# Conditional residual chain on one core: second gates and their difference in other slots, residual folded ahead of x's split, another order behind the last product

## The chip, the cores and the metric

The kernel runs on one core of one Trainium2 chip. The metric is the device time of one execution in microseconds (us); lower is better. Engines are named as in the profile: PE (TensorE) multiplies, DVE (VectorE) and ACT (ScalarE) work on tiles, POOL (GpSimd) folds residuals and issues accumulating DMAs, SP (SyncE) issues most other DMAs. A `q` behind a name means that engine's sequencer, which issues DMAs and waits.

## The reference

Four conditional layers, each added to its input, for eight sequences of 256 tokens and 1024 channels, all in float32:

```python
# L0: one weight W for all, plus a mixture of 8 rank-16 experts, top 2 by logits
logits = x @ Wr.T + 5 * one_hot(lang)         # per token
gates  = softmax over the two largest logits, 0 elsewhere
x = x + x @ W.T + 2 * sum_e gates[e] * (x @ A[e].T) @ B[e].T
# L1: a mask of signs per sequence
x = x + x @ W1.T + b1 + coeff[b] * (x @ (2 * mask[b] - 1))
# L2: one of 8 full weights per sequence
x = x + x @ W2[ids[b]].T
# L3: one of 8 rank-16 adapters per sequence
x = x + 16/16 * (x @ B3[ids[b]].T) @ A3[ids[b]].T
```

## The kernel before

**Split products.** Every float32 operand is split into a high part (`whi`, `ghi`, a cast to fp32r on ACT) and a low part (`wlo`, `glo`, the difference, on DVE). A product is hi·hi + hi·lo + lo·hi on PE. The residual "x +" is folded into the weights: `fold_block` adds the identity to a diagonal 128x128 block, so that x @ (W + I) comes out of PE.

**Order of the work.** The schedule is written by hand: each engine executes its instructions in the order in which the program emits them. The work is a list of slots. There are two passes, g=0 and g=1, each over two pairs of sequences, p0 and p1. A pass begins with the 16 slots of L0 (`l0_slot`), then come units of L1 and L2 (`unit_slot`), 64 in a pass. In L0 the 2x2 block product of both pairs is made with seven block products instead of eight (sums `S1` to `S4` of weight blocks, `T1` to `T4` of x blocks), two slots for each product. The parts C11, U1, V, W, C12, C22 and C21 leave PSUM in `l0_evacuate` (DVE row `c<-mm,c`, two tiles t=0, 1 of two column blocks each); slots 10 to 15 keep adding in the same PSUM banks after C12 has been read at the start of slot 12.

**What a slot emits.** In `l0_slot`, in this order: evacuations of earlier sums, the works listed for `-s`, the high parts of the items four ahead (`highs`, ACT), residual folds (`fold`, POOL), the low parts (`lows`, DVE), the works listed for `s`, merges of L1's weights (`merge_add`, POOL), PE's own products (`l0_main`), and last `merge_scale` (ACT, L257, which turns an int32 mask tile into scaled floats). Lists of works are built in `l0_works` with `at(slot, ...)`; a negative slot means ahead of that slot's high and low parts. High parts have five buffers and low parts four, so those of a slot can begin only when PE has finished the slot before.

**The gates.** `gates_by_rank(p)` brings the gates of a pair into the layout of ranks and tokens (tile `gt`). `gate(p)` multiplies them with the experts' hidden values from PSUM (DVE, `gt<-ph,gt`). `split_gates` makes `ghi` (ACT, L401) and `glo` (DVE). `gate_difference(g)` subtracts the second pair's from the first's (DVE, `gt<-gt,gt`) and splits the result. PE uses them as extra terms of products (`lora`): p1's in slots 9 and 13, the difference in slot 15.

**The head.** `head()` is slots 0 and 1 of the first pass, where everything waits for the first loads. It goes in four blocks (m = 2s + k): cast and split 512 columns of x, fold and cast and split 512 columns of `A11`, multiply, then experts on the same operand. SP's first issues (L1013 to L1020) bring x, `A11` and the experts' `la` in that order, before larger loads. Nine warm-up matmuls (L998) run meanwhile.

**The end.** After the last unit, L3 of the last sequence is left: `proj` (x times B3, PE), `sums` (row `pr`, which adds up four partial groups), `third` (its split `rt`, ACT and DVE), and the last product with A3, eight column blocks of 128 channels. `fill(2)` works off two pieces of the sequence before (`pf` on PE, an addition on DVE; the stores in `store()`). The residual of channels 4 to 7 is put into PSUM by PE with an identity matrix (L1050, L1055) and copied out by ACT (L1067); that of channels 0 to 3 is added by DVE (L1065). The stores are issued by SP, the last one of ACT's half by ACT (L1068 to L1070). `bank(n)` is one of four single PSUM banks, `ps.tile` a pair of banks.

Of the kernel before, what the change touches and what calls it, by code (L numbers as in the profile page):

```python
# [8 lines left out]
F32 = mybir.dt.float32  # L9
# [3 lines left out]
ALU = mybir.AluOpType  # L13
AX = mybir.AxisListType

P = 128
NB = 8
T = 256
N = 2 * T
# [15 lines left out]
def kernel(ctx: ExitStack, tc: tile.TileContext, x, lang, coeff, ids,  # L35
# [31 lines left out]
    def tt(o, a, b, op):  # L67
        nc.vector.tensor_tensor(o, a, b, op)  # L68
# [124 lines left out]
    def source(n):  # L193
        kind, q, m, j = items[n]
        if kind == "L0":
            return quad(q, m)[j]
        r = raws[n]
        return (f32(r) if kind == "L1" else r)
# [34 lines left out]
    def fold_block(t, eng=None):  # L233

        (eng or nc.gpsimd).tensor_tensor(t, t, ident, ALU.add)  # L235
# [37 lines left out]
    def prep_hi(n):  # L273
        if n not in his:
            his[n] = wp.tile([P, 1024], FR, tag="whi", name=f"whi{n}", bufs=HI_AHEAD + 1)
        return his[n]

    def prep_lo(n):
        if n not in los:
            los[n] = wp.tile([P, 1024], FR, tag="wlo", name=f"wlo{n}", bufs=LO_AHEAD + 1)  # L280
        return los[n]
# [116 lines left out]
    def split_gates(key, gt):  # L398
        hi = gp.tile([P, N], FR, tag="ghi", name="ghi", bufs=2)
        lo = gp.tile([P, N], FR, tag="glo", name="glo", bufs=2)  # L400
        copy(hi, gt)  # L401
        tt(lo, gt, f32(hi), ALU.subtract)
        gates[key] = hi, lo

    def gate(p):
        tt(gts[p], phs.pop(p), gts[p], ALU.mult)

    def gate_difference(g):

        a, b = (gts.pop(pair_of(g, j)) for j in range(2))  # L410
        tt(a, a, b, ALU.subtract)
        split_gates(("diff", g), a)
# [206 lines left out]
    def experts(g, p, n, k, kk):  # L619

        if k == 0:
            phs[p] = bank(3 - p % 2, f"ph{p}")
        v = [t.rearrange("p (k c) -> p k c", k=2) for t in (his[n], los[n])]
        hi, lo = (t[:, k % 4, :] for t in la_w[g, k // 4])
        mm(phs[p], hi, v[0][:, kk], start=(k == 0), stop=False)  # L625
        mm(phs[p], hi, v[1][:, kk], start=False, stop=False)  # L626
        mm(phs[p], lo, v[0][:, kk], start=False, stop=(k == K - 1))  # L627
# [14 lines left out]
    def la_parts(g, k0, k1):  # L642

        h = k0 // 4
        if (g, h) not in la_w:
            la_w[g, h] = [gp.tile([P, 4, P], FR, tag=tag, name=f"la{tag}", bufs=2)
                          for tag in ("ghi", "glo")]
        k = slice(k0 - 4 * h, k1 - 4 * h)
        raw = LA[g][:, k0:k1]
        hi, lo = la_w[g, h]  # L650
        copy(hi[:, k], raw)
        tt(lo[:, k], raw, f32(hi[:, k]), ALU.subtract)
# [16 lines left out]
    def l0_works(g):  # L669


        p0, p1 = pair_of(g, 0), pair_of(g, 1)
        w = {}

        def at(s, *fs):
            w.setdefault(s, []).extend(fs)

        def add(name, h, src):
            nc.gpsimd.dma_start(quad(g, name)[h], src, accum_op=ALU.add)

        def s1_add(h):
            fold_quad(quad(g, "S1")[h], h)
            add("S1", h, w0[1, 2 + h])

        def s3_add(h):
            t = quad(g, "S3")[h]
            copy(flat(t), flat(quad(g, "S2")[h]))
            fold_quad(t, h)
            add("S3", h, w0[1, 2 + h])

        def s4_add(h):
            copy(flat(quad(g, "S4")[h]), flat(quad(g, "S2")[h]))
            add("S4", h, w0[0, 2 + h])

        def less(h, name, j, i):

            t = flat(quad(g, name)[h])
            nc.scalar.mul(t, t, -1.0)
            add(name, h, x[pair_of(g, j)][:, 4 * i + 2 * h:4 * i + 2 * h + 2])

        def both(f, *args):
            return [lambda h=h: f(h, *args) for h in range(2)]

        def subs(o, a, b):
            return [lambda h=h: sub(g, o, a, b, h) for h in range(2)]

        def lb_parts():
            copy(lbs[0], lb_raw)
            tt(lbs[1], lb_raw, f32(lbs[0]), ALU.subtract)

        if g == 0:
            at(1, constants, *both(s1_add))
            at(2, *both(less, "T1", 1, 0), lambda: router([p0]))
            at(3, lambda: weigh([p0]), lambda: expand(p0), lb_parts, *subs("S2", "A11", "S1"))
            at(4, *both(s4_add), lambda: gate(p0))
            at(5, lambda: router([p1]))
            at(6, lambda: weigh([p1]), lambda: expand(p1))
        else:
            at(0, *both(s1_add), *both(less, "T1", 1, 0))
            at(2, lambda: expand(p0))  # L720
            at(3, *subs("S2", "A11", "S1"))
            at(4, *both(s4_add), lambda: gate(p0))
            at(5, lambda: expand(p1))
        at(-5, lambda: split_gates(p0, gts[p0]))
        at(4, *both(less, "T3", 1, 1))
        t2 = subs("T2", "T1", "B22")
        at(7, t2[0], *both(s3_add))
        at(8, t2[1], lambda: gate(p1), lambda: split_gates(p1, gts[p1]))
        at(11, lambda: gate_difference(g))
        for h in range(2):  # L730
            at(9 + h, lambda h=h: add("T4", h, x[p0][:, 4 + 2 * h:6 + 2 * h]))
        for i in range(4):
            at(12 + i, lambda i=i: split_c(p1, i))
        return w
# [90 lines left out]
    def head():  # L825

        chain(0, 0)
        for s in range(2):
            for k in range(2):
                parts = [(2 * s, 512 * k, 512 * k + 512), (2 * s + 1, 512 * k, 512 * k + 512)]  # L830
                if s + k == 0:
                    parts[1:] = [(1, 0, 256), (1, 256, 512)]
                for i, c0, c1 in parts:
                    m = 2 * s + k
                    if i % 2 and c0 <= 512 * k + m * P < c1:
                        fold_block(W0[0, "A11", s][:, k, m * P:(m + 1) * P], nc.vector)
                    c = slice(c0, c1)
                    copy(prep_hi(i)[:, c], flat(source(i))[:, c])  # L838
                    tt(prep_lo(i)[:, c], flat(source(i))[:, c], f32(his[i])[:, c],
                       ALU.subtract)  # L840
                la_parts(0, 2 * s + k, 2 * s + k + 1)
                if (s, k) == (1, 1):
                    leave = logits(1)
                    highs(4)
                    leave()
                product(s, 0, [k], start=(s == 0))
                experts(0, 1, 2 * s, 2 * s + k, k)
            folded.update((2 * s, 2 * s + 1))
        by_token(1)


# [160 lines left out]
    for h in range(2):  # L1012
        for k in range(2):  # L1013
            m = 2 * h + k
            load_x(0, 0, m, m + 1)
            for c in ((slice(0, 256), slice(256, 512)) if m == 0 else (slice(0, 512),)):
                nc.sync.dma_start(W0[0, "A11", h][:, k, c], w0[0, h][:, k, c])
            if m % 2 == 0:
                k0, k1 = m, m + 2
                nc.sync.dma_start(LA[0][:, k0:k1], la[:, k0:k1])  # L1020
# [20 lines left out]


    b = NB - 1
    proj(b, 1, 1)
    at = l3[b]
    xt = xts[b]
    half = K // 2
    tiles = [ps.tile([P, 2, N], F32, tag="mm", name=f"po{b}_{i}") for i in range(2)]
    ends = {half + m: tiles[m // 2][:, m % 2, :T] for m in range(half)}
    mm(ends[half], ident, xt[:, half, :], start=True, stop=False)  # L1050
    fill(2)
    store()
    sums.pop(b)()
    for m in range(half + 1, K):
        mm(ends[m], ident, xt[:, m, :], start=True, stop=False)  # L1055
    rt = third(b)
    firsts = bank(0, f"po{b}_0"), bank(2, f"po{b}_2")
    for m in range(half):
        for po, m2 in ((firsts[m // 2][:, m % 2 * T:m % 2 * T + T], m),
                       (ends[half + m], half + m)):  # L1060
            mm(po, at[:, m2 * P:(m2 + 1) * P], rt, start=(m2 < half), stop=True)

    for m0, m1 in ((0, 1), (1, 2), (2, 4)):
        xs = xt[:, m0:m1, :].rearrange("p m t -> p (m t)")
        tt(xs, firsts[m0 // 2][:, m0 % 2 * T:m0 % 2 * T + T * (m1 - m0)], xs, ALU.add)  # L1065
        for m in range(m0, m1):
            copy(xt[:, half + m, :], ends[half + m])  # L1067
        nc.sync.dma_start(out[b, :, m0:m1, :], xt[:, m0:m1, :])  # L1068
        queue = nc.scalar if m1 == half else nc.sync
        queue.dma_start(out[b, :, half + m0:half + m1, :], xt[:, half + m0:half + m1, :])  # L1070


# [55 lines left out]
```

## Time and profile before

| | us |
|---|---|
| median of three runs | 607.04 |
| lowest and highest run | 606.71, 608.16 |
| profiled execution, its own time | 608.14 |
| its span, first to last instruction | 605.9 |
| PE busy | 596.5 |
| DVE busy | 473.8 |
| ACT busy | 385.5 |
| POOL busy | 129.7 |
| mean granted PE clock | 0.999 |

A row of the timeline or of the chain of waits gives the start and the length in us, then engine, line, operation, tiles and shapes, and in brackets how long the engine was idle before it and what ended that. Matmul rows overlap, because PE works on several at once; the distance between their starts is their price: about 0.227 us for 128x512 in fp32r. Two-pass float32 matmuls show two rows each. L68 is the helper `tt`, which makes every DVE tensor-tensor operation, so these are told apart by their tiles. DMA rows on a queue are the time of issuing; the landing comes later.

### The profile page before, as it was taken

What the parts mean: (1) busy time and instruction counts of PE and PEld (TensorE: products, weight loads), DVE (VectorE), ACT (ScalarE), POOL (GpSimd) and SP (SyncE); (2) the same over time, 40 slices, a digit from 0 to 9 for tenths busy, and PEclk for the clock granted to TensorE, in tenths of its full rate; (3) what the DMA queues carried; (4) which work ended last, traced back from release to release, by engine and by line L of the source; (5) the groups of instructions that cost most, each with busy time, mean ns of one, the idle gap of its engine ahead of it and who ended that gap; (6) DMA issues with size and microseconds to landing.
All of it is one profiled execution on the core that took longest, in us unless ns stands there. A gap on an engine that the chain in (4) does not pass through costs nothing.

```text
span 605.9 us, 8943 instructions
## 1 busy us (share of the span) xinstructions
PE 596.5 (98%) x3244; PEld 499.7 (82%) x3244; DVE 473.8 (78%) x557; ACT 385.5 (64%) x456; POOL 129.7 (21%) x174
## 2 busy tenths in 40 slices
PE   8999999999999999999999999999999999999996
PEld 7777778888888888888778878788888888888885
DVE  5579688899699899586655785879968999977853
ACT  4667465687569797543553864658866788764431
POOL 0322250114121114122110224500422110421100
PEclk9999999999999999999999999999999999999999
DMA  8977794467684767599940799936757686747503
GB/s 282 341 192 167 167 241 149 176 229 269 203 301 179 269 249 277 209 350 321 269 70 20 164 248 209 266 104 209 278 196 256 209 285 236 290 161 235 184 1 138
DMA packets 39821, 130.22 MB, mean 215 GB/s; under 512 B 4834, under 2 KB 7010, under 8 KB 39010
## 3 DMA queue, kind: packets, MB, share of 16 engines
q1 hardware_dynamic: 35026, 112.62, 52.6%
q0 software_dynamic: 4608, 16.78, 15.3%
q8 instruction: 25, 0.41, 0.3%
q10 hardware_dynamic: 144, 0.26, 0.1%
q14 instruction: 18, 0.15, 0.1%
HBM read 121.25 MB, written 8.39 MB: 214 GB/s over the span
## 4 chain that ended last, share of the span: by engine, by line
PE 89%; DVE 4%; DMA 3%; issue 2%; ACT 2%; SPq 0%; DVEq 0%; ACTq 0%
PE po L531 38%; PE mm L599 23%; PE po L540 20%; DVE wlo L68 2%; DMA A<-in_w 2%; PE pf L470 1%; PE pb L442 1%; DMA x<-in_x 1%; PE pl L308 1%; PE ph L626 1%; PE ph L627 1%; PE ph L625 1%; DVE c L68 1%; DVE gt L68 1%; ACT ghi L401 0%
## 5 line engine op out<-in xcount | busy, mean ns | idle before, releaser
L531 PE MATMUL po<-hl,whi 128*128 128x512 f32 x1016 | 254.5, 392 | 0.0
L531 PEld LDWEIGHTS po<-hl,whi 128*128 128x128 f32 x1016 | 182.8, 189 | 32.7
L68 DVE TENSOR_TENSOR wlo<-raw,whi 128x1024 fp32r<-128x1024 f32 x128 | 160.6, 1265 | 1.1 <-issue 1.1
L540 PEld LDWEIGHTS po<-hl,wlo 128*128 128x128 f32 x1016 | 137.6, 190 | 11.3 <-issue 1.6
L288 ACT CAST whi<-raw 128x1024 fp32r<-128x1024 f32 x128 | 133.8, 1048 | 18.1 <-PE mm L599 8.4
L540 PE MATMUL po<-hl,wlo 128*128 128x256 f32 x1016 | 142.3, 283 | 0.0
L599 PE MATMUL mm<-whi,whi 128*128 128x512 f32 x224 | 88.9, 397 | 1.1 <-DVE c L68 0.9
L599 PE MATMUL mm<-wlo,whi 128*128 128x512 f32 x224 | 87.9, 392 | 0.0
L257 ACT ACTIVATE raw<-raw,negc,c 128x1024 f32<-128x1024 int32 x64 | 79.6, 1243 | 4.7 <-DMA raw<-in_mask 4.7
L235 POOL TENSOR_TENSOR raw<-raw,ident 128x128 f32<-128x128 f32 x72 | 54.0, 753 | 120.8 <-DMA raw<-in_w 96.8
L599 PE MATMUL mm<-whi,wlo 128*128 128x512 f32 x224 | 71.0, 392 | 0.0
L68 DVE TENSOR_TENSOR raw<-raw,w 128x1024 f32<-128x1024 f32 x56 | 69.0, 1231 | 1.9 <-issue 1.9
L235 POOL TENSOR_TENSOR w<-w,ident 128x128 f32<-128x128 f32 x28 | 31.1, 1109 | 168.4 <-DMA w<-in_w 118.3
L68 DVE TENSOR_TENSOR wlo<-x,whi 128x1024 fp32r<-128x1024 f32 (+1 forms) x38 | 45.6, 1210 | 16.2 <-issue 8.6
L599 PEld LDWEIGHTS mm<-whi,whi 128*128 128x128 f32 x224 | 42.3, 189 | 13.0 <-ACT raw L257 1.6
L599 PEld LDWEIGHTS mm<-whi,wlo 128*128 128x128 f32 x224 | 42.2, 188 | 9.5 <-DVE wlo L68 0.4
L288 ACT CAST whi<-A 128x1024 fp32r<-128x1024 f32 x26 | 27.3, 1051 | 35.3 <-PE mm L599 17.7
L599 PEld LDWEIGHTS mm<-wlo,whi 128*128 128x128 f32 x224 | 42.3, 189 | 8.6
L572 ACT COPY c<-po 128x512 f32<-128x512 f32 (+1 forms) x34 | 18.8, 552 | 45.9 <-PE po L540 45.9
L288 ACT CAST whi<-x 128x1024 fp32r<-128x1024 f32 x34 | 35.3, 1049 | 11.1 <-PE mm L599 8.8
L575 ACT ACTIVATE sum<-po,b_sb 128x512 f32<-128x512 f32 (+1 forms) x36 | 23.0, 640 | 28.7 <-PE po L540 28.7
L68 DVE TENSOR_TENSOR wlo<-A,whi 128x1024 fp32r<-128x1024 f32 (+2 forms) x31 | 35.6, 1151 | 4.3 <-ACT whi L838 2.5
(126 smaller groups left out, 516.2 us busy)
## 6 DMA issues: line engine op xcount, KB each, us to landing
raw<-in_mask SPq DMA_DIRECT2D x64, 512.0 KB, 5.4
raw<-in_w SPq DMA_DIRECT2D x64, 512.0 KB, 4.7
w<-in_w SPq DMA_DIRECT2D x28, 512.0 KB, 3.4
out<-c SPq DMA_DIRECT2D x29, 256.0 KB, 2.8
A<-in_w SPq DMA_DIRECT2D x14, 512.0 KB, 8.7
x<-in_x SPq DMA_DIRECT2D x6, 1024.0 KB, 8.0
A<-in_w POOLq DMA_DIRECT2D x12, 512.0 KB, 8.5
x<-in_x POOLq DMA_DIRECT2D x12, 512.0 KB, 8.3
```

What stands on the lines that cost most here:

```text
L68: nc.vector.tensor_tensor(o, a, b, op)
L235: (eng or nc.gpsimd).tensor_tensor(t, t, ident, ALU.add)
L257: nc.scalar.activation(f32(raws[n]), raws[n], AF.Identity, bias=negc[:, b:b + 1], scale=c2[:, b:b + 1])
L288: copy(prep_hi(i), flat(source(i)))
L308: mm(pl[c:c + 32, :], wrs[:, k, :], X[g][:, j, k, :], start=(k < 4), stop=(k >= 4))
L442: mm(pb[c:c + 32, j * T:(j + 1) * T], l3b[b][:, k, :], xts[b][:, k, :], start=(k < 4), stop=(k >= 4))
L470: mm(po[:, i * T:(i + 1) * T], at[:, (m + i) * P:(m + i + 1) * P], rt, start=True, stop=True)
L531: mm(po, hi[:, c], xhl[:, k, j].rearrange("p h t -> p (h t)"), start=(k == 0), stop=False)
L540: mm(po[:, :T], lo[:, c], xhl[:, k, j, 0, :], start=False, stop=(k == K - 1))
L572: copy(xs, po[:, :, T:])
L575: nc.scalar.activation(xs, po[:, :, T:], AF.Identity, bias=b1c)
L599: mm(*args, skip_group_check=True, **kw)
```

## The change

Three places. In `l0_works`, `gate(p1)` moves ahead of slot 8's high and low parts, the split of its result ahead of the second half of T2's difference, and the gate difference from slot 11 to slot 10. In `head`, the fold of the residual block is put ahead of x's low part in the first block, and A's columns are cast and split in halves of 256 in all four blocks (before: in the first only); the first block of `A11` is loaded in one transfer instead of two. At the end, the identity copies are made for channels 6 and 7 alone, after `fill`, `store` and `sums`; channels 0 to 5 are added by DVE from three single banks; the column blocks are multiplied in the order 0, 6, 7, 1, 2, 3, 4, 5; and ACT issues two stores of 256 KB, SP three.

```diff
@@ l0_works
-        at(8, t2[1], lambda: gate(p1), lambda: split_gates(p1, gts[p1]))
-        at(11, lambda: gate_difference(g))
+        at(-8, lambda: gate(p1))
+        at(8, lambda: split_gates(p1, gts[p1]), t2[1])
+        at(10, lambda: gate_difference(g))
@@ head
         for s in range(2):
+            v, w = 2 * s, 2 * s + 1
+
+            def high(i, k, c0=0, c1=512):
+                c = slice(512 * k + c0, 512 * k + c1)
+                copy(prep_hi(i)[:, c], flat(source(i))[:, c])
+
+            def low(i, k, c0=0, c1=512):
+                c = slice(512 * k + c0, 512 * k + c1)
+                tt(prep_lo(i)[:, c], flat(source(i))[:, c], f32(his[i])[:, c], ALU.subtract)
+
             for k in range(2):
-                parts = [(2 * s, 512 * k, 512 * k + 512), (2 * s + 1, 512 * k, 512 * k + 512)]
-                if s + k == 0:
-                    parts[1:] = [(1, 0, 256), (1, 256, 512)]
-                for i, c0, c1 in parts:
-                    m = 2 * s + k
-                    if i % 2 and c0 <= 512 * k + m * P < c1:
-                        fold_block(W0[0, "A11", s][:, k, m * P:(m + 1) * P], nc.vector)
-                    c = slice(c0, c1)
-                    copy(prep_hi(i)[:, c], flat(source(i))[:, c])
-                    tt(prep_lo(i)[:, c], flat(source(i))[:, c], f32(his[i])[:, c],
-                       ALU.subtract)
-                la_parts(0, 2 * s + k, 2 * s + k + 1)
-                if (s, k) == (1, 1):
+                m = 2 * s + k
+                block = W0[0, "A11", s][:, k, m * P:(m + 1) * P]
+                high(v, k)
+                if m:
+                    low(v, k)
+                fold_block(block, nc.vector)
+                high(w, k, 0, 256)
+                high(w, k, 256)
+                if not m:
+                    low(v, k)
+                low(w, k, 0, 256)
+                low(w, k, 256)
+                la_parts(0, m, m + 1)
+                if m == 3:
                     leave = logits(1)
                     highs(4)
                     leave()
...
@@ first loads
             load_x(0, 0, m, m + 1)
-            for c in ((slice(0, 256), slice(256, 512)) if m == 0 else (slice(0, 512),)):
-                nc.sync.dma_start(W0[0, "A11", h][:, k, c], w0[0, h][:, k, c])
+            nc.sync.dma_start(W0[0, "A11", h][:, k], w0[0, h][:, k])
@@ end
     b = NB - 1
+    at, xt = l3[b], xts[b]
     proj(b, 1, 1)
-    at = l3[b]
-    xt = xts[b]
-    half = K // 2
-    tiles = [ps.tile([P, 2, N], F32, tag="mm", name=f"po{b}_{i}") for i in range(2)]
-    ends = {half + m: tiles[m // 2][:, m % 2, :T] for m in range(half)}
-    mm(ends[half], ident, xt[:, half, :], start=True, stop=False)
     fill(2)
     store()
     sums.pop(b)()
-    for m in range(half + 1, K):
-        mm(ends[m], ident, xt[:, m, :], start=True, stop=False)
+    ends = ps.tile([P, 2, N], F32, tag="mm", name="ends")
+    by_act = (K - 2, K - 1)
+    for i, m in enumerate(by_act):
+        mm(ends[:, i, :T], ident, xt[:, m, :], start=True, stop=False)
     rt = third(b)
-    firsts = bank(0, f"po{b}_0"), bank(2, f"po{b}_2")
-    for m in range(half):
-        for po, m2 in ((firsts[m // 2][:, m % 2 * T:m % 2 * T + T], m),
-                       (ends[half + m], half + m)):
-            mm(po, at[:, m2 * P:(m2 + 1) * P], rt, start=(m2 < half), stop=True)
-
-    for m0, m1 in ((0, 1), (1, 2), (2, 4)):
+    leave = [bank(n, f"po{b}_{n}") for n in (0, 2, 1)]
+
+    def place(m):
+        return ends[:, m % 2, :T] if m in by_act else leave[m // 2][:, m % 2 * T:m % 2 * T + T]
+
+    for m in (0, *by_act, 1, 2, 3, 4, 5):
+        mm(place(m), at[:, m * P:(m + 1) * P], rt, start=(m not in by_act), stop=True)
+
+    for m0, m1, queue in ((0, 1, nc.sync), (1, 2, nc.sync), (2, 4, nc.sync), (4, 6, nc.scalar)):
+        if m0 == 4:
+            for i, m in enumerate(by_act):
+                copy(xt[:, m, :], ends[:, i, :T])
+            nc.scalar.dma_start(out[b, :, K - 2:K, :], xt[:, K - 2:K, :])
         xs = xt[:, m0:m1, :].rearrange("p m t -> p (m t)")
-        tt(xs, firsts[m0 // 2][:, m0 % 2 * T:m0 % 2 * T + T * (m1 - m0)], xs, ALU.add)
-        for m in range(m0, m1):
-            copy(xt[:, half + m, :], ends[half + m])
-        nc.sync.dma_start(out[b, :, m0:m1, :], xt[:, m0:m1, :])
-        queue = nc.scalar if m1 == half else nc.sync
-        queue.dma_start(out[b, :, half + m0:half + m1, :], xt[:, half + m0:half + m1, :])
+        tt(xs, leave[m0 // 2][:, m0 % 2 * T:m0 % 2 * T + T * (m1 - m0)], xs, ALU.add)
+        queue.dma_start(out[b, :, m0:m1, :], xt[:, m0:m1, :])
```

More of the change, by code (lines that the diff above doesn't have):

```diff
@@ L846, in head @@
                 product(s, 0, [k], start=(s == 0))
-                experts(0, 1, 2 * s, 2 * s + k, k)
-            folded.update((2 * s, 2 * s + 1))
+                experts(0, 1, v, m, k)
+            folded.update((v, w))
         by_token(1)
```

## Prediction, made before the change was run

> **What bounds the kernel now.** I read the page's busy shares and its chain first, to see whether anything but TensorE sets the time:
>
> ```profile
> PE 596.5 (98%) x3244; PEld 499.7 (82%) x3244; DVE 473.8 (78%) x557; ACT 385.5 (64%) x456; POOL 129.7 (21%) x174
> PE 89%; DVE 4%; DMA 3%; issue 2%; ACT 2%; SPq 0%; DVEq 0%; ACTq 0%
> ```
>
> TensorE is the bound nearly everywhere, and the change leaves its work alone apart from two small copies at the very end. So it can pay only where TensorE waits, or before its start and after its end. Second, the waits of TensorE's matmuls (total, times, longest) over the whole span:
>
> ```profile
> PE mm L599 <- ACT ghi L401: 0.9, 2, 0.5
> PE mm L599 <- DVE c L68: 0.9, 2, 0.4
> ```
>
> Two kinds of wait, each once per pass (g=0, g=1), and both belong to what is moved. Third, the chain of waits inside the first pass (start, length, what):
>
> ```profile
> 65.40 0.61 DVE gt L68
> 66.01 0.02 issue
> 66.03 0.63 ACT ghi L401
> 66.66 0.04 issue
> 66.70 11.29 PE mm L599 x47
> ...
> 84.93 0.69 DVE glo L68
> 85.62 1.14 DVE c L68
> 86.77 0.14 issue
> 86.90 5.25 PE mm L599 x22
> ```
>
> See who stands in front of TensorE: in slot 9 the gates' high part, made last in slot 8's works; at slot 12 the evacuation `c` of C12, held on VectorE's queue behind the gate difference. The time lost is read from the starts of the matmuls, not from the listed idle, since a late low part stretches the rows after it:
>
> ```profile
> 65.71 0.61 PE L599 MATMUL mm<-whi,wlo 128*128 128x512 f32 x2
> 66.70 0.73 PE L599 MATMUL mm<-ghi,lb 128*128 128x512 f32 x2 [0.38 <-ACT ghi L401]
> 67.43 0.50 PE L599 MATMUL mm<-glo,lb 128*128 128x512 f32 x1
> 67.77 0.40 PE L599 MATMUL mm<-whi,whi 128*128 128x512 f32 x1
> ```
>
> From 65.71 to 67.77 are five starts; the same five one column block later (68.72 to 69.87) take 1.15 us, here 2.06: 0.91 us lost. Last, the head (ScalarE's cast of the second block of A, then TensorE's first and third matmul on it), and the last store to be issued:
>
> ```profile
> 9.53 0.62 ACT L838 CAST whi<-A 128x512 fp32r<-128x512 f32 x1 [0.96 <-DVE A L235]
> ...
> 10.21 0.50 PE L599 MATMUL mm<-whi,whi 128*128 128x512 f32 x1
> ...
> 10.93 0.49 PE L599 MATMUL mm<-whi,wlo 128*128 128x512 f32 x1
> ```
>
> ```profile
> 601.85 0.46 SPq L1068 DMA_DIRECT2D out<-c  x1
> ```
>
> **Second pair's gates, slot 8.** VectorE's order was: two `c`, two low parts (1.14 us each), the T2 difference (1.14), gate (0.61), then ScalarE's `ghi` (0.63) and VectorE's `glo` (0.69). New: `c` ends at 61.91, gate to 62.5, low parts to 64.8, `glo` to 65.4, T2 to 66.55. ScalarE is free from 62.3, so `ghi` is there at 63.2. TensorE comes to slot 9 at 65.71 + 2x0.227 = 66.16 and asks for `glo` at 66.6. The wait goes, with 1.2 us to spare. What is pushed back: slot 9's low parts by 0.6 us (ready 64.8, wanted from 66.4), and T2, whose cast starts at 68.64 now and, with slot 9 earlier, at 67.2 (T2 ready 66.55). The int32 scaling (L257) queued behind `ghi` comes earlier. Saved: 0.91 us, and 1.01 in the second pass (359.91 to 362.07 is 2.16 for 1.15).
>
> **Gate difference, slot 11 to 10.** At slot 12 the starts 85.86 and 87.21 are three apart: 1.35 instead of 0.68, 0.67 lost; 0.66 in the second pass. VectorE has a hole from 79.12 to 80.67 in slot 10, where nothing can be split until TensorE frees a buffer. The difference goes there: 79.1 to 79.7 (0.69, or 1.01 as it was beside GpSimd's fold), `ghi` to 80.35, `glo` to 81.05. Slot 11's first low part slips from 80.67 to 81.05. Then C12's first evacuation waits only for TensorE's second column block (83.6 + 0.3): 83.9 to 85.1, against 86.31 where slot 12 wants the bank: 1.2 us to spare. The price is on ScalarE, in order: `ghi` now waits there until 79.7, so L257 slips from 77.13 to 80.35, and slot 11's cast of `A` from 80.66 to 81.5, its low part to 82.5-83.7; that lies in the spare time. GpSimd's fold of that raw tile slips from 80.78 to about 81.6, its accumulating DMA with it (10.0 us to landing); first casts of raw tiles come at 101.54, so 9 us cover it. T4's DMA in slot 10 waits for a low part that ends before the difference starts, so it stays; SP's queue is not passed. What is late next, if that cover were gone, is again `c` at slot 12, one for one.
>
> Gates together: 0.91+1.01+0.67+0.66 = 3.25; I take 3.1, since a switch of operands may keep a few hundredths each.
>
> **Head.** SP issues one transfer instead of two for the first block of A: everything behind it goes out 0.45 us earlier, until issues wait for older transfers to land (8.62 waits for a landing, for one). The two halves landed at 4.1 and 4.5; the whole lands at about 4.5. VectorE then folds at 4.5-4.8 instead of after x's low part (5.04-5.32). That would start TensorE at 5.3 instead of 5.81, but the warm-up matmuls hold it until 5.58: 0.2 us earlier. The rows there start 0.43 us apart until 7.25, and 0.227 after 7.6. The Trainium skill, "TensorE: Matmul & The Clock Gate", Part 1, says that the array runs at half rate until a free-running window of 3.4 us has been busy; by it an earlier start only puts more matmuls at half rate, and the switch moves by some 0.5 us from run to run whatever the change. By the start alone the sum would hold 0.2; by the rule, with the switch at a fixed time, 0.2 x 0.227/0.43 = 0.1. I take 0.1. At the second block the cast in halves counts: two halves take 0.71 us, so the first is out 0.36 us after 9.53, at 9.9 instead of 10.15, its low part (0.42) at 10.3 instead of 10.88. TensorE lost 0.08 before 10.21 and 0.38 until 11.27 (1.06 for three starts): 0.46, all gone. Sum 0.5; bounds 0.1 (landings decide) and 0.9 (landings 0.4 us earlier too). Later blocks are ready over 1 us before use, which covers the 0.09 us that halves cost on ScalarE. The shift survives: ScalarE's and VectorE's next jobs start on TensorE's releases, and the loads behind them have landed (A12 at 15.9, its cast at 19.95).
>
> **Tail.** TensorE's copies of four residual blocks (0.43 us each) become two, and the first no longer stands before `fill(2)`. Now: first copy 596.06, `pf` 596.41, VectorE's two `pf` additions 597.04-598.33, `rt` 598.36-598.78, last product 598.83. New: `pf` at 596.1, additions 596.7-598.0, `rt` to 598.45, product at 598.5: 0.33 us earlier. SP then had five issues of 0.48 us each, first 599.94, last 601.85. New: SP 599.6, 600.0, 600.5; ScalarE copies two blocks by 599.8, issues 599.9, and its second at 601.15 behind VectorE's fourth addition. By issues the end comes 0.7 us earlier. The trace says the engines were 0.85, 0.98 and 0.88 busy from 601 to 604 at 292 to 351 GB/s. The skill, "DMA: Bandwidth & Descriptors", Issuing engines are not separate DMA queues, speaks against the second queue: it saves only issue time, the same 16 engines carry the bytes. By bytes (1.05 MB at 340 GB/s, 3.1 us from 0.85 us after the first issue) the end moves with the first issue: 0.33. I take the middle, 0.5, because the engines were only 0.27 busy from 600 to 601, so earlier issues can fill some of that; bounds 0.2 and 0.8.
>
> **Sum.** 3.1 + 0.5 + 0.5 = 4.1 us. The profiled execution took 608.14 (span 605.9 and 2.2 around it) and lies at the top of 606.71 to 608.16; the median is 607.04. Its span should become 601.8; from the median, 602.9. No change can be told here within 0.3%, 1.8 us.
>
> **The rivals.** (A) One of the two gate waits is refilled by what is queued next: the `c` additions or low parts are slower beside GpSimd (1.22 becomes 1.49 at 81.82, 2.49 at 87.81). Against it, spare time is 1.2 us at both places. Kept: half of 3.1, so 604.5. (B) The head follows the landings and the tail the bytes: 0.1 + 0.3 + 3.1, so 603.6. For it: DMA is 0.95 to 1.07 busy from 7 to 12. (C) Both gate waits are refilled: only 1.0 is left, 606.0, no change. (D) Slower: ScalarE's queue. `ghi` in slot 10 blocks it until VectorE's difference is done, and L257, both casts of slot 11, their low parts and then C12's evacuation follow. It decides beyond 1.2 us of slip, one for one, twice; to eat the 4.1 and 1.8 more, `ghi` must be late by 1.2 + 5.9/2, over 4 us, in each pass: 609. VectorE would have to be stretched past double for that; its rows in 76 to 80 are 1.22. Nor can the change miss its aim: both waits name the moved instructions.
>
> **How the numbers follow.** All parts pay 0.65 (602.9); A 0.14; B 0.09; C 0.07; D 0.05. Faster 0.65+0.14+0.09 = 0.88, same 0.07, slower 0.05. The range takes main case, A and B with the bounds: low 3.25+0.9+0.8 and half a microsecond of run spread (1.45 between the runs shown), 601.5; high A with a small head and tail (0.1 and 0.2), 605.2.
>
> **What would show it.** Right: slot 9 with no idle before `mm<-ghi`; the difference's row in the hole of slot 10, `c` of slot 12 split into two rows with a wait on TensorE before the second; 0.227 us starts from the second block of the head; last issue near the old 601.85 less 4.3, on ScalarE's queue. Wrong: a new idle before L599 at slots 9 to 13, ScalarE's casts of slot 11 over 2 us late, or TensorE's start at 5.8 again.

## The result: 3.9 us faster, and the profile after

| | before | after |
|---|---|---|
| median of six runs, us | 607.35 | 603.41 |
| lowest and highest run | 606.71, 608.16 | 602.74, 605.13 |
| ratio (95% interval) | | 0.9937 [0.9921, 0.9952] |
| profiled execution, its own time | 608.14 | 603.36 |
| its span | 605.9 | 601.0 |

The gain is 3.9 us by the runs and 4.9 us by the pair of traces; where the difference between the two comes from is told further down. The page of after, busy shares and chain:

```profile
PE 593.1 (99%) x3240; PEld 499.1 (83%) x3240; DVE 474.2 (79%) x561; ACT 385.7 (64%) x457; POOL 135.2 (23%) x174
PE 97%; ACT 1%; DVE 1%; issue 0%; DVEq 0%; POOL 0%; POOLq 0%; ACTq 0%
```

No engine was given less to do, apart from four fewer rows on PE (two float32 identity copies, two rows each). DVE has four more rows. What went is time in which PE got no further. The page books 3.4 us of it as less busy time of PE and 1.5 us as less idle time, since rows that waited for a late operand were stretched and counted as busy, and the four rows at the end are gone. Of the waits of PE (total, times, longest), the two rows that carried the forecast are absent, and no other row of L599 waiting for ACT or DVE has come in their place. These are left:

```profile
PE warm L1010 <- POOL ident masks.py:199: 1.4, 1, 1.4
PE ph L626 <- DVE wlo L68: 0.3, 1, 0.3
PE po L1071 <- DVE rt L68: 0.3, 1, 0.3
```

Slot 9 in the timeline of PE (start, length; a row with x2 holds two starts):

```profile
64.97 0.62 PE L599 MATMUL mm<-whi,wlo 128*128 128x512 f32 x2
65.44 0.63 PE L599 MATMUL mm<-ghi,lb 128*128 128x512 f32 x2
65.91 0.39 PE L599 MATMUL mm<-glo,lb 128*128 128x512 f32 x1
66.14 0.40 PE L599 MATMUL mm<-whi,whi 128*128 128x512 f32 x1
```

The same five starts that took 2.06 us now take 66.14 - 64.97 = 1.17, with no bracket, so no wait. Slots 10 to 12 on DVE show why the second wait went too:

```profile
77.40 0.95 DVE L68 TENSOR_TENSOR gt<-gt,gt 128x512 f32<-128x512 f32 x1
79.04 0.69 DVE L68 TENSOR_TENSOR glo<-gt,ghi 128x512 fp32r<-128x512 f32 x1 [0.69 <-ACT ghi L401]
...
82.27 1.22 DVE L68 TENSOR_TENSOR c<-mm,c 128x1024 f32<-128x1024 f32 x1
84.87 1.23 DVE L68 TENSOR_TENSOR c<-mm,c 128x1024 f32<-128x1024 f32 x1 [1.38 <-PE mm L599]
```

The gate difference and its low part lie in the former hole of slot 10. C12's first evacuation now ends at 83.5, and the second one waits for PE (the bracket) instead of PE for it.

To find where the 4.9 us lie I took the start of the same matmul in both traces, step by step down the program. The lead of after grows at these places:

| stretch | lead at its end, us | gained in it |
|---|---|---|
| first product of the head (5.81 to 5.43) | 0.38 | 0.38 |
| rest of the head, to slot 7 of the first pass | 0.72 | 0.34 |
| slot 9, first pass | 1.65 | 0.93 |
| slot 12, first pass | 2.33 | 0.68 |
| second pass, before its slot 7 | 2.83 | 0.50 |
| slot 9, second pass | 3.84 | 1.01 |
| slot 12, second pass, until the last `proj` | 4.53 | 0.69 |
| the end | 4.87 | 0.34 |

Gates 3.31, head 0.72, end 0.34, and 0.50 at a place that the change does not touch.

### The profile page after: what moved, and what is told of

The parts are those of the page before. It is cut to its first block, busy times and chain, and to the rows that moved or that the text cites. A ratio compares the mean times of both kernels' runs of the same rounds, so it can differ in the third digit from the quotient of the medians.

```text
span 601.0 us, 8936 instructions
## 1 busy us (share of the span) xinstructions
PE 593.1 (99%) x3240; PEld 499.1 (83%) x3240; DVE 474.2 (79%) x561; ACT 385.7 (64%) x457; POOL 135.2 (23%) x174
## 4 chain that ended last, share of the span: by engine, by line
PE 97%; ACT 1%; DVE 1%; issue 0%; DVEq 0%; POOL 0%; POOLq 0%; ACTq 0%
PE po L531 39%; PE mm L599 30%; PE po L540 20%; PE pl L308 1%; PE pf L470 1%; PE pb L442 1%; PE ph L626 1%; PE ph L627 1%; PE ph L625 1%; PE warm L1010 1%; PE pb L489 0%; ACT x L698 0%; DVE c L68 0%; PE po L548 0%; PE pg L392 0%
## 5 line engine op out<-in xcount | busy, mean ns | idle before, releaser
L599 PE MATMUL mm<-whi,whi 128*128 128x512 f32 x224 | 88.6, 396 | 0.0
L599 PE MATMUL mm<-wlo,whi 128*128 128x512 f32 x224 | 87.9, 392 | 0.0
L235 POOL TENSOR_TENSOR raw<-raw,ident 128x128 f32<-128x128 f32 x72 | 60.5, 843 | 115.6 <-DMA raw<-in_w 100.8
L257 ACT ACTIVATE raw<-raw,negc,c 128x1024 f32<-128x1024 int32 x64 | 79.5, 1242 | 3.9 <-DMA raw<-in_mask 3.9
L599 PE MATMUL mm<-whi,wlo 128*128 128x512 f32 x224 | 70.8, 391 | 0.0
L599 PEld LDWEIGHTS mm<-whi,whi 128*128 128x128 f32 x224 | 42.2, 189 | 11.1 <-issue 1.1
L599 PEld LDWEIGHTS mm<-whi,wlo 128*128 128x128 f32 x224 | 42.2, 188 | 9.2 <-DVE wlo L68 0.2
L599 PEld LDWEIGHTS mm<-wlo,whi 128*128 128x128 f32 x224 | 42.2, 188 | 8.6
L68 DVE TENSOR_TENSOR c<-mm,c 128x1024 f32<-128x1024 f32 x20 | 24.4, 1221 | 21.8 <-PE mm L599 21.8
```

The costliest lines, as they stand in the source:

```text
L257: nc.scalar.activation(f32(raws[n]), raws[n], AF.Identity, bias=negc[:, b:b + 1], scale=c2[:, b:b + 1])
L599: mm(*args, skip_group_check=True, **kw)
```

## The experiments

**Each part alone.** The change has three parts in different places, so each was put on the kernel before by itself; a fourth run moves the gates of slot 8 and leaves the difference in slot 11.

```diff
 gates only (e1)
-        at(8, t2[1], lambda: gate(p1), lambda: split_gates(p1, gts[p1]))
-        at(11, lambda: gate_difference(g))
+        at(-8, lambda: gate(p1))
+        at(8, lambda: split_gates(p1, gts[p1]), t2[1])
+        at(10, lambda: gate_difference(g))
 head only (e2): the edits of head() and of the first loads, nothing else
 end only (e3): the edits behind the last product, nothing else
 slot 8 only (e4): as e1, but
+        at(11, lambda: gate_difference(g))
```

Gates only: 

> The kernel before with only the three lines of the gates changed (gate of p1 ahead of slot 8's parts, its split ahead of T2's second half, the difference in slot 10). Theory: the four waits of TensorE at slots 9 and 12 are independent of head and tail, so the trace loses 0.9 + 0.7 in the first pass and 1.0 + 0.7 in the second: span 605.9 - 3.3 = 602.6, time 607.3 - 3.3 = 604.0. Rival 1 (a wait is refilled where the head is late): half of it, 605.7. Rival 2 (the 0.5 us that the changed kernel's trace gains between 296 and 312, on the load of la for the second pass, belongs to the moved gates): 603.5. If instead that load only jitters, the gain there comes or goes at random between these runs.

Head only: 

> The kernel before with only the head changed (one load of the first block of A, fold ahead of x's low part in the first block, casts and splits in halves in all four). Theory: TensorE reaches slot 2's products 0.7 us earlier and keeps it: span 605.2, time 606.6, and the starts come down to 0.23 us apart by about 6.8 us, not 7.3. Rival (the head's lead is used up by a later wait, on a load or on the gates of p0 at slot 5): below 0.2 us at the end, 607.2.

End only: 

> The kernel before with only the end changed (two identity copies instead of four, product order 0 6 7 1 2 3 4 5, stores by two queues). By bytes: the end follows the first store's issue, 0.4 us, span 605.5, time 606.95. By issues: it follows the last store's issue, 0.7 us, span 605.2, time 606.65. A rival that the tail gives nothing (the last store's landing is the same): 607.3.

Slot 8 only: 

> The kernel before with the second pair's gate and split moved in slot 8, the difference left in slot 11. Theory: the waits at slot 9 go (0.9 and 1.0), the waits at slot 12 stay at 0.7 each: span 604.0, time 605.4. Rival (TensorE's earlier start of slot 9 makes the wait at slot 12 longer, since VectorE's list of slot 11 then ends later against it): the wait at slot 12 grows to over 1.0 and the gain is below 1.3, time 606.0.

| run | median, us | ratio to before (95%) | span | slot 7 to slot 13, first pass | same, second pass |
|---|---|---|---|---|---|
| before | 608.09 | 1 | 605.9 | 35.06 | 41.02 |
| gates only | 604.38 | 0.9938 [0.9919, 0.9957] | 601.0 | 33.32 | 39.28 |
| slot 8 only | 605.61 | 0.9960 [0.9942, 0.9977] | 603.6 | 34.01 | 39.99 |
| head only | 607.55 | 0.9995 [0.9983, 1.0007] | 605.0 | 35.05 | 41.05 |
| end only | 607.30 | 0.9991 [0.9979, 1.0004] | 604.3 | 35.05 | 41.05 |
| whole change | 603.41 | 0.9937 [0.9921, 0.9952] | 601.0 | 33.45 | 39.32 |

The median of before in this table was taken beside the four runs; its span and stretches are of the trace shown at the start, and the ratio of the whole change is to its own before, 607.35. The last two columns run from the same matmul of `pg` in slot 7 to the first `ghi` product of slot 13. They hold only the gates' two places, and head and end leave them alone to 0.03 us. Slot 8 alone takes 1.05 and 1.03 off them, gates only 1.74 in each pass, the whole change 1.61 and 1.70 (why 0.13 less in the first pass is open). So both moves pay, each at its own place. In the waits of PE of slot 8 only, the row of `ghi` is gone and this one has stayed:

```profile
PE mm L599 <- DVE c L68: 0.9, 2, 0.4
```

In head only both rows have stayed:

```profile
PE mm L599 <- ACT ghi L401: 0.9, 2, 0.5
PE mm L599 <- DVE c L68: 0.9, 2, 0.4
```

Head and end alone are too small to be told from no change by their runs: the intervals of both contain 1, head only came to 607.55 where 606.6 was expected, and gates only gains nearly as much by its runs (3.7 us) as the whole change (3.9). Their size has to come from the traces.

**What in the head pays.** Two runs take one thing out of the changed head: the halves of A's columns behind the first block (e5), and the fold ahead of x's low part (e6). e7 puts all stores of the end on SP; in the head it is the same as after.

```diff
 whole columns again behind the first block (e5)
-                high(w, k, 0, 256)
-                high(w, k, 256)
+                cuts = ((0, 512),) if m else ((0, 256), (256, 512))
+                for cut in cuts:
+                    high(w, k, *cut)
 (the same for low)
 fold behind x's low part again (e6)
                 high(v, k)
-                if m:
-                    low(v, k)
+                low(v, k)
                 fold_block(block, nc.vector)
...
-                if not m:
-                    low(v, k)
```

> The changed kernel with A cast and split in one piece in blocks two to four of the head (halves kept in the first). Theory (the halves take TensorE's stall at the second block away): the second block's first three matmuls come 0.33 and 0.39 us apart again, as in the three traces of whole casts that are not held by TensorE itself, 0.25 to 0.4 us lost there; everything else as in the changed kernel. Rival (the block is reached late anyway because the half-rate matmuls of the first block last longer): starts 0.23 us apart, nothing lost.

> The changed kernel with the first block's fold behind x's low part again (one load and halves kept). Theory: the fold then starts at about 4.9 instead of 4.64 and TensorE's first product at 5.6 to 5.7 instead of 5.4; of these 0.2 to 0.3 us nothing or 0.1 is left at the second block, which waits for its own loads. Rival (the earlier fold is what shortens the head): the second block's first product moves by the same 0.2 to 0.3.

One execution each: 604.62 (whole columns) and 603.11 (fold behind), spans 602.1 and 600.8. The head is read from five times in each trace: the first product, the first start that the next one follows 0.23 us later (full rate), the start of x's low part in the second block (it follows the landing of that block of x by about 0.7 us), and the first `pl`, with which the head ends; the last column is the distance between these two.

| run | A's columns, blocks 2 to 4 | first product | full rate from | second block of x | `pl` | last two |
|---|---|---|---|---|---|---|
| before | whole | 5.81 | 7.62 | 8.61 | 17.48 | 8.87 |
| end only (e3) | whole | 5.77 | 6.11 | 7.81 | 16.71 | 8.90 |
| slot 8 only (e4) | whole | 5.71 | 6.05 | 8.27 | 17.18 | 8.91 |
| e5 | whole | 5.66 | 7.48 | 8.43 | 17.34 | 8.91 |
| after | halves | 5.43 | 6.75 | 8.20 | 16.63 | 8.43 |
| e6 | halves | 5.99 | 6.44 | 8.15 | 16.59 | 8.44 |
| e7 | halves | 5.42 | 6.41 | 8.07 | 16.50 | 8.43 |
| gates only (e1) | whole | 5.63 | 6.98 | 7.53 | 16.61 | 9.08 |
| head only (e2) | halves | 5.41 | 7.60 | 7.55 | 16.80 | 9.25 |

In the seven upper rows PE waits for the data of the second block, and the last column has two values only: about 8.90 with whole columns, 8.43 with halves. Three more traces with halves, of runs that come further down, give 8.42 (e9), 8.44 (e10) and 8.42 (e11). So the halves are worth 0.46 us where PE waits for the second block. The fold's place is worth nothing here: with it put back, the first product is later by 0.56 us (5.99 against 5.43) and `pl` is not (16.59 against 16.63). In the two lower rows the second block had landed early, and in e2 the full rate came late as well: PE itself was late then, and halves could not help. The second block of the head, in after and then in e5:

```profile
9.12 0.71 ACT L834 CAST whi<-A 128x256 fp32r<-128x256 f32 x2 [0.96 <-DVE A L235]
9.58 0.50 PE L599 MATMUL mm<-whi,whi 128*128 128x512 f32 x1
...
10.15 0.39 PE L599 MATMUL mm<-whi,wlo 128*128 128x512 f32 x1
```

```profile
9.36 0.62 ACT L834 CAST whi<-A 128x512 fp32r<-128x512 f32 x1 [0.96 <-DVE A L235]
...
10.03 0.50 PE L599 MATMUL mm<-whi,whi 128*128 128x512 f32 x1
...
10.76 0.50 PE L599 MATMUL mm<-whi,wlo 128*128 128x512 f32 x1
```

In after the cast is in two halves. The first `mm` starts 0.46 us after the cast begins (0.67 in e5, 0.68 in before), and the third one 0.57 us after the first (0.73 and 0.72). No landing is earlier for the one transfer in place of two: the low part of x's second block starts at 8.06 on average in four traces with the old loads and at 8.06 in eight with the new, between 7.53 and 8.61.

**The stores of the end (e7).** Both queues against one:

```diff
-    for m0, m1, queue in ((0, 1, nc.sync), (1, 2, nc.sync), (2, 4, nc.sync), (4, 6, nc.scalar)):
+    for m0, m1, queue in ((0, 1, nc.sync), (1, 2, nc.sync), (2, 4, nc.sync), (4, 6, nc.sync)):
...
-            nc.scalar.dma_start(out[b, :, K - 2:K, :], xt[:, K - 2:K, :])
+            nc.sync.dma_start(out[b, :, K - 2:K, :], xt[:, K - 2:K, :])
```

> The changed kernel with all five last stores issued by SP. From the last projection's last matmul to the end of the span the kernel before takes 10.9 us, the changed one 10.5. By issues: the last store is issued 0.5 us later than now, so 10.9 to 11.0. By bytes: first store at the same time, end 10.5 to 10.7.

603.29 in one execution, span 601.1. From the first matmul of the last `proj` (`pb` in the timeline) to the end of the span it is 10.91 to 10.99 in the four traces with the old end, 10.53 to 10.61 in seven with the new one (10.58 in after), and 10.89 here: of the 0.36 us that the new end gains on average, nearly all is lost again. The issues of the end in after, and then in e7:

```profile
595.09 1.41 SPq L1080 DMA_DIRECT2D out<-c  x3
595.20 0.37 ACTq L1077 DMA_DIRECT2D out<-c  x1
596.62 0.34 ACTq L1080 DMA_DIRECT2D out<-c  x1
```

```profile
594.85 1.30 SPq L1080 DMA_DIRECT2D out<-c  x3
596.24 0.41 SPq L1077 DMA_DIRECT2D out<-c  x1
596.74 0.41 SPq L1080 DMA_DIRECT2D out<-c  x1
```

After issues ACT's first store 0.11 us behind SP's first; in e7 it comes 1.39 us behind it. Counted from `pb`, the first store goes out at the same time in both (4.64), the last one 0.36 later in e7. So it is the second queue that pays, some 0.3 us, and not the new order of the products by itself.

**How much spare time C12's evacuation has (e9).** Rival D and rival A rest on the 1.2 us of slot 12. This run puts work in front of it: slot 11's low part of `A` is made three times instead of once, so two further subtractions of 128x1024 stand ahead of `c` on DVE. They write the same values again.

```diff
         at(10, lambda: gate_difference(g))
+
+        def again():
+            i = first[slot_of[g, 11]] + LO_AHEAD
+            tt(prep_lo(i), flat(source(i)), f32(his[i]), ALU.subtract)
+
+        at(11, *[again] * 2)
```

> The changed kernel with two more VectorE operations in slot 11 (the low part of slot 12's A made again, twice, 1.14 us each), in the place that the gate difference had. Theory: 1.2 us is spare ahead of slot 12, so C12's first evacuation ends about 1.1 us late and TensorE waits 1.0 to 1.2 us at slot 12 in each pass: span 2.2 us longer than without them. Rival (TensorE's wait there was set by ScalarE's split and not by VectorE's queue): no wait at slot 12, same span.

609.07 in one execution, span 606.7: 5.7 us more than after, where I had expected about 2.2. DVE, then PE, in slots 11 and 12 of the first pass:

```profile
80.91 4.74 DVE L68 TENSOR_TENSOR wlo<-A,whi 128x1024 fp32r<-128x1024 f32 x3 [0.26 <-ACT whi L288]
85.58 2.34 DVE L68 TENSOR_TENSOR c<-mm,c 128x1024 f32<-128x1024 f32 x2
```

```profile
84.00 0.61 PE L599 MATMUL mm<-whi,wlo 128*128 128x512 f32 x2
86.94 0.77 PE L599 MATMUL mm<-whi,whi 128*128 128x512 f32 x1 [2.32 <-DVE c L68]
87.50 0.63 PE L599 MATMUL mm<-wlo,whi 128*128 128x512 f32 x1
87.93 0.63 PE L599 MATMUL mm<-whi,whi 128*128 128x512 f32 x1
```

Two things were larger than I had counted. The three subtractions take 4.74 us, some 1.56 each from start to start instead of 1.14, and the slow ones have GpSimd's folds beside them (POOL is busy the whole of 82 to 84 in the windows below). The second of the three by itself:

```profile
82.17 2.08 DVE L68 TENSOR_TENSOR wlo<-A,whi 128x1024 fp32r<-128x1024 f32 x1
```

That GpSimd is the cause rests on more than this place: in before, after and e9 every low part of this size that took over 1.3 us had POOL busy beside it (33, 29 and 32 rows), and every one without POOL took 1.21 to 1.23. More than half of those beside POOL are not slow, though; what tells them apart is open. So `c` is 3.5 us later than in after, and PE stands still: the start that was due at 84.46 comes at 86.94, 2.48 us late. Then the starts are 0.43 apart instead of 0.227. The windows (length, then busy time of PE, PEld, DVE, ACT and POOL, then the granted clock, the share of DMA and GB/s) show why:

```profile
82.00:84.00 2.00, 2.00 (x10) 1.66 (x9) 1.97 (x2) 0.97 (x1) 2.00 (x4) 1.00 0.98 262
84.00:86.00 2.00, 0.62 (x3) 0.19 (x1) 1.97 (x3) 1.67 (x2) 1.59 (x3) 1.00 1.05 209
86.00:88.00 2.00, 1.06 (x3) 0.90 (x4) 2.00 (x3) 1.50 (x3) 1.17 (x3) 0.65 1.09 215
88.00:90.00 2.00, 2.00 (x6) 1.59 (x5) 2.00 (x2) 1.02 (x1) 0.00 (x0) 0.50 1.04 246
90.00:92.00 2.00, 2.00 (x10) 1.62 (x9) 1.33 (x2) 0.00 (x0) 0.00 (x0) 1.00 1.05 274
```

The granted clock (last column but two) falls to 0.50 at 86.6, while PE still stands, and is back at 90.0. The whole loss of the first pass, by the starts of the same matmul here and in after, is 4.02 us: the gap and some 1.5 us of half rate. In the second pass the same edit makes `c` 2.82 late and PE waits only 1.61:

```profile
382.36 0.47 PE L599 MATMUL mm<-whi,whi 128*128 128x512 f32 x1 [1.61 <-DVE c L68]
```

There the clock stays, and 1.88 is lost. What was taken up without loss is 3.5 - 2.48 = 1.0 in the first pass and 2.82 - 1.88 = 0.94 in the second: this is the spare time of slot 12.

**A further step (e10), with after run again beside it (e11).** In after, PE still waits 0.3 us for a low part in slot 2 of the first pass (`ph`, in its waits above), and in slot 5 two starts of `ghi` and `glo` stand too far apart. e10 makes the low parts of the items four ahead right behind their high parts at the end of the head, and puts the difference T3 one slot later in the first pass. e11 is after, unchanged.

```diff
 e10
                     highs(4)
+                    lows(4)
                     leave()
...
-        at(4, *both(less, "T3", 1, 1))
+        at(5 - g, *both(less, "T3", 1, 1))
```

> The changed kernel once more, as the reference for the next one on the same chip and for another trace of the same head. Theory: ratio 0.993 to 0.995; the head's length differs by up to 0.8 us from the first trace of it, since the clock's step to full rate and the landing of the second block of x fall at other times; the gates' waits stay away.

> The changed kernel with two more moves in the first pass: the low part of slot 2's x made in the head (VectorE is idle there) instead of behind the experts' low parts, and the negation of x for T3 (two ScalarE operations, 1.9 us, with their accumulating DMAs) in slot 5 instead of slot 4, behind the split of p0's gates. Theory: TensorE's waits at slot 2 (0.3 to 0.7 us) and at slot 5 (0.5 us) go, 0.8 to 1.2 us in all, and nothing else waits: ratio to the kernel before 0.992. Rival (T3's sums land late, or ScalarE's list of slot 5 is then too long for slot 6): a new wait of TensorE in slots 6 to 12, no gain over the changed kernel.

| run | median, us | lowest and highest | ratio to before (607.6 on this chip) | span |
|---|---|---|---|---|
| after again (e11) | 603.90 | 603.41, 605.54 | 0.9940 [0.9925, 0.9954] | 601.9 |
| e10 | 603.12 | 602.12, 603.55 | 0.9924 [0.9910, 0.9937] | 599.8 |

The two intervals overlap, so that e10 beats after is likely and not shown. Its wait in slot 2 is gone, and slot 5 runs evenly, but behind slot 5 a new wait stands, for ACT's copy of C11. The row is of PE's weight loads, and the two starts after it are 0.46 us apart instead of 0.23:

```profile
PEld mm L599 <- ACT c L744: 0.5, 1, 0.5
```

```profile
46.75 0.39 PE L599 MATMUL mm<-glo,lb 128*128 128x512 f32 x1
47.21 0.49 PE L599 MATMUL mm<-whi,whi 128*128 128x512 f32 x1
```

In the stretch with slots 5 and 6 the net gain is 0.2 us, where a stall of 0.6 had been removed. Here a wait did take the place of the removed one.

## Why the prediction was right, step by step

**Gates: 3.1 forecast, 3.31 measured.** The terms were 0.91, 1.01, 0.67 and 0.66; the stretches show 0.93, 1.01, 0.68 and 0.69. The four terms sum to 3.25, and the forecast put 3.1 without saying why; the 0.15 taken off was not needed. The orders worked out also hold: with the lead of 0.72 at slot 7 and 1.65 behind slot 9 taken into account, `gate`, `glo`, the difference, L257 and the cast of `A` lie within about 0.3 us of where they were put. The slip on ScalarE that was the price of the move was really paid, and hidden: its L257 of slot 10 starts only behind `ghi`, on time for slot 11:

```profile
78.39 0.62 ACT L401 CAST ghi<-gt 128x512 fp32r<-128x512 f32 x1 [2.80 <-DVE gt L68]
78.91 1.24 ACT L257 ACTIVATE raw<-raw,negc,c 128x1024 f32<-128x1024 int32 x1
80.06 1.04 ACT L288 CAST whi<-A 128x1024 fp32r<-128x1024 f32 x1
```

**The spare time: 1.2 forecast at slot 12, 1.0 and 0.94 measured (e9).** The forecast counted up to PE's start; in after `c` ends at 83.49 and PE starts at 84.67, 1.18 later, but in e9 some 0.2 us lie between the end of `c` and the start that waited for it. The error is too small to have decided anything, and rival A did not come. But the price of rival D beyond that point, "one for one", was too low: in the first pass the gap of 2.48 us brought some 1.5 us of half rate on top. So it was not D's mechanism but its price that was mis-sized. That ScalarE's `ghi` itself were late was not tried; e9 delays the same evacuation from VectorE's side.

**Head: 0.5 forecast, made of 0.46 for the halves and 0.1 for the earlier start.** The 0.46 is what the traces above give (8.90 against 8.43). For the earlier start nothing is to be seen: TensorE starts at 5.41 to 5.43 in after, e2 and e7 instead of 5.63 to 5.81, yet e6 starts at 5.99 and loses nothing. With the same first block as after, e5 starts at 5.66, so the start varies by itself as much as the change was to move it. The upper bound, landings 0.4 us earlier, is not borne out by the mean of 8.06 in both groups: in this part issues that went out earlier did not land earlier, as rival B had it. What the forecast had not in its sum is the spread of the head itself. In ten of the twelve traces `pl` follows x's second block by one of the two distances above, so the spread is that of the landing. The clock's step moves far more than the 0.5 us that the forecast named (see the last section), but it had a part in the length of the head only where the block came early (e2). The mean of `pl` is 17.00 in the four traces with the old head and 16.62 in five with the whole new one (after, e2, e7, e9, e11), 0.38 apart, inside a spread of 0.9 in the old ones. Before's own trace had the longest head of all: of the 0.85 us between its `pl` and that of after, 0.41 is the later second block of x. This is why the pair of traces shows 0.72 for the head. Its runs alone give head only 0.9995, which fits 0.4 us as well as it fits none.

**The 0.50 that no step had.** It comes at the `pt` products between the passes, where ACT's cast waits for the load of `la` for the second pass. This row of before

```profile
295.42 0.62 ACT L651 CAST laghi<-c 128x512 fp32r<-128x512 f32 x1 [2.10 <-DMA c<-in_la]
```

has become a shorter wait in after (1.46), but in after run again it is longer than before, and now PE waits too:

```profile
293.42 0.62 ACT L651 CAST laghi<-c 128x512 fp32r<-128x512 f32 x1 [2.40 <-DMA c<-in_la]
...
296.04 1.14 PE L319 MATMUL pt<-ident,lg 128*128 128x128 f32 x8 [0.81 <-ACT lg L312]
```

From the second pass's `pl` to its `pt` it is 6.67 us in before, 7.44 in e11, and 6.47 in the ten other traces, e2 and e3 among them, which leave the gates alone. So this is the landing of a load, and neither the change nor the moved gates. The later second block of x (0.41) and this load (0.50) make up most of the 1 us by which the pair of traces (4.9) goes beyond the runs (3.9): the traced execution of before, 608.14, was 0.8 us above the median.

**End: 0.5 forecast, 0.36 measured on average (0.34 in the pair of traces).** The estimate was the middle between 0.33, if the bytes decide, and 0.7, if the issues do. The measured figure is that of the bytes, but by luck: if the bytes alone decided, e7, whose first store goes out at the same time, would have ended after 10.5 to 10.7, and it took 10.89. So the issues count, which the forecast had right by half. The Trainium skill ("DMA: Bandwidth & Descriptors", Issuing engines are not separate DMA queues) allows a second queue only the time of issuing and calls that usually small beside the transfer; it was this time that was saved, and at the end nothing hid it. The last issue, at 596.62, is 0.7 us earlier than in before, counted from `pb`, but only half of that arrives at the end. The rest is most likely lost to the DMA engines. One window of after, in its last DMA stretch, shows these full (share 1.03) with every other engine idle:

```profile
597.00:598.00 1.00, 0.00 (x0) 0.00 (x0) 0.00 (x0) 0.00 (x0) 0.00 (x0) 0.55 1.03 357
```

**The sum.** 3.31 for the gates, about 0.4 for the head and 0.36 for the end are 4.1, the sum that was forecast; that it fits so well is in part luck, since the gates gave 0.2 more than forecast and head and end each 0.1 less. The runs gave 3.9 and 603.4 us against 602.9. More than half of that distance is the median of before, from which the forecast counted: it was 607.04 over three runs and is 607.35 over six, and 608.09 beside the four runs of the parts. As a number, 603.4 lies nearer to rival B's 603.6, but as a gain 3.9 lies nearer to 4.1 than to B's 3.5; of B's two claims, the landings did decide the head, and the bytes alone did not decide the end.

## What to carry to other kernels

Look for the queue in front of a waiting bound engine: two waits of 0.5 and 0.4 us in a list of totals were worth 0.93 and 0.68 us per pass by the distance of the starts, and moving work of the same length into a hole on the same queue took all of it. Before moving work, work out the spare time of whatever then becomes last, and count beyond it with more than one for one, since a gap of TensorE can cost its clock too (it did in one pass of e9 and not in the other). For parts of half a microsecond, compare stretches inside several traces: here their runs could not tell 0.4 us from nothing, and one pair of traces was 1 us off, mostly through the landing of two loads.

## What the runs showed of the hardware

- **The clock changes on a grid of 3.41 us, and a step need not be idle for it to fall.** In e9 an idle time of 2.32 us took the granted clock to 0.50, one of 1.61 us did not. In all twelve traces the time between two changes of the granted clock is a whole number of steps of 3.413 us: 24, 1 and 150 steps in e9, 173 to 175 in the others. Where the steps lie differs from run to run. Three of them in e9:

```profile
83.18:86.59 3.41, 1.44 (x7) 0.86 (x5) 3.38 (x3) 1.99 (x2) 3.00 (x5) 1.00 1.08 229
86.59:90.00 3.41, 3.06 (x7) 2.49 (x8) 3.41 (x4) 2.19 (x2) 0.58 (x2) 0.50 1.05 232
380.14:383.55 3.41, 1.80 (x8) 1.23 (x7) 3.41 (x4) 3.09 (x4) 3.00 (x5) 1.00 1.06 211
```

The first held 1.44 us of PE's work, and the clock fell at its end; the third held 1.80, and the clock stayed. The ends of the traces, where PE runs out of work, fit this: over all twelve traces the clock fell after every step with up to 1.46 us of work (12 cases) and after none with 2.0 or more; in between, it fell after one with 1.93. So the border is near half a step, roughly, since PE's busy time is modelled. From PE's last row to the fall it took 1.2 (e9) to 4.8 us (before), so 1.61 us is not safe everywhere. The Trainium skill, "TensorE: Matmul & The Clock Gate", Part 1, gives one idle window of about 3.4 us, free-running, for this; the length agrees, but the window was not idle here, and the measurement decides.
- **The clock's first step moves.** With the same start of the warm-up (1.37 or 1.38 us) the granted clock rose between 4.38 (e3) and 7.53 us (before), 3.15 us apart, nearly a whole step of that grid. The step before each rise held 3.0 us of PE's work or more, the one before that 2.7 at most, as the rule that the forecast drew on has it. The same page gives half a microsecond to either side.
- **VectorE beside GpSimd.** A subtraction of 128x1024 took 1.21 to 1.23 us without GpSimd beside it, and up to 2.08 (e9) and 2.49 us (before, at 87.81) with its folds beside it.
- **Issues that go out 0.45 us earlier did not land earlier** among the first loads: x's second block was taken up at 8.06 us on average either way, with a spread of 1.1 us.
